# Parts of Q and K written to DRAM once, two groups later, and read twice by the fills of the stacks

## The chip, the cores and the metric

The kernel runs on one core of a Trainium2 chip. The metric is the device time of one launch in microseconds, as the median of several runs. All data are float32 in DRAM. The engines that matter are TensorE (PE in the profile: matrix products, with weight loads as PEld), VectorE (DVE), ScalarE (ACT), GpSimd (POOL) and SyncE (SP), whose instructions here issue DMA transfers. ScalarE can issue DMA transfers too. The 16 DMA engines of the core carry them out.

## The reference

The reference is one post-norm transformer layer on x of shape (8, 1024, 256): attention with 16 heads of 16 elements and a fixed bias, then a feed-forward layer with ternary weights and a low-rank addition.

```python
Q = split_heads(x @ Wq.T + bq); K = split_heads(x @ Wk.T + bk); V = split_heads(x @ Wv.T + bv)
scores = einsum('bhqd,bhkd->bhqk', Q, K) / sqrt(16) + prior_lambda * _gaussian_mask(1024)
out = einsum('bhqk,bhkd->bhqd', softmax(scores), V)
x = layernorm(x + out.reshape(8, 1024, 256) @ Wo.T + bo)
h = bitlinear(x, w_fc) + gate * (x @ v.T @ fast_b.T @ u.T)
x = layernorm(x + bitlinear(relu(h) ** 2, w_proj))
```

## The kernel before

Products are made at float32 precision out of a faster, shorter type (float32r). Each of Q and K is split into two parts, a rounded part and the rest, held in the tile `two` (L629 to L631: ScalarE rounds, GpSimd subtracts). A score is then one product over 64 rows: for each of 16 elements of the head, four rows pair the parts of K with the parts of Q in all four ways. In K the four rows are part 0, part 1, part 0, part 1. In Q they are part 0, part 1, part 1, part 0.

These 64 rows are the *stacks* (L290): for each pair of heads `pr` and each member `a` of the pair, one tile for K and one for Q, 64 partitions of 1024 float32 values. Member `a` = 0 uses partitions 0 to 63, member 1 partitions 64 to 127. The other partitions hold zeros, and two rows for the row maxima. There are two slots, so that one head group of four heads is used while the next one's stacks are filled.

The way from `two` to a stack goes through DRAM. `write_parts` (L199) writes the parts into `parts_of`, a DRAM tile of 128 rows (8 heads of 16 elements), four copies and 1024 columns; `fill_one` (L313) reads the 16 rows of one head, four copies each, into the 64 partitions of a stack. `fill_stack` (L321) makes the eight fills of a head group, K and Q in turn, all on the SP queue. Only the very first head group is filled in halves, part of it on ScalarE's queue, and its parts are written for the low 64 rows first (L244 to L339).

The main loop (L1508) runs over 512 groups, 16 for a head group and 64 for a batch. A group g makes the exponentials of two tiles (`exp_scores`, L751) and the maximum of rows for the scores that are used 12 groups later (`max_scores`, L652, with `max_row` on VectorE, L674). Every 16 groups, at the loop's head, `fill_stack` asks for the next head group; its first scores are made 4 groups later. Every 8 groups `set_max` (L688) turns the maxima, and sends them through DRAM (`rows`) into the Q stacks by one write and four copies (L702, L709). The exponentials need them 3 groups later. All engines follow the order in which the program is written (L1632 to L1637); among the DMAs of one queue this order holds as well.

Beside that, a list of pieces of other work is spread over the groups: making Q and K of the next heads (`queries_keys`, L602), V, and the feed-forward layer of the batch before. `defer(n, f)` (L383) puts f at the end of the group n groups later. At the end of a head group the weighted sums go to DRAM (`raw_o` and `sums`, L812, L815). When the third and the fourth head group of a batch are done, `normalize` (L822) fetches the sums (`den`, one group later), inverts them on VectorE (three groups later, L834), writes them back (`back`, L836) and reads them repeated 16 times (`rec`, L841: the source lists 8 rows, each repeated for 16 partitions).

Of the kernel before, what the change touches and what calls it, by code (L numbers as in the profile page):

```python
# [10 lines left out]
F32 = mybir.dt.float32  # L11
# [6 lines left out]
P = 128  # L18
HD = 16
HG = 4  # L20
VW = HD + 1
HALF = 512
# [21 lines left out]
def tile_postln_layer(  # L44
# [20 lines left out]
    nc = tc.nc  # L65
    B, L, D = x.shape
# [29 lines left out]
    def big(name):  # L96
        return epool.tile([P, 2 * HALF], F32, tag="e", name=name)
# [12 lines left out]
    for name, w in (("k", wk), ("q", wq), ("v", wv), ("o", wo)):  # L110
        t = big(f"raw_{name}")[:, : NDC * D].rearrange("p (c d) -> p c d", d=D)
# [3 lines left out]
    for name, src in (("k", bk), ("q", bq)):  # L115
        t = cpool.tile([P, NDC], F32, tag=f"b{name}", name=f"b{name}")
# [74 lines left out]
    parts_of, made = {}, {}  # L191

    def new_parts(name, b, c):
        parts_of[name, b, c] = dpool.tile(
            [P, 4, L], F32, tag=f"parts_{name}", name=f"parts_{name}_{b}_{c}"
        )
        return parts_of[name, b, c]

    def write_parts(name, t, two, half, rows=slice(0, P)):  # L199
        to, two = t[rows, :, ts(half, HALF)], two[rows].bitcast(F32)  # L200
        nc.sync.dma_start(to[:, :2], two)
        if name == "k":
            nc.sync.dma_start(to[:, 2:], two)
        else:
            nc.sync.dma_start(to[:, 2, :], two[:, 1, :])
            nc.sync.dma_start(to[:, 3, :], two[:, 0, :])

    def first_part(name, half, two):
        pt = bank0(f"p{name}_0_0_{half}")
# [20 lines left out]
    for name in "kq":  # L230
        new_parts(name, 0, 0)
# [4 lines left out]
    two = {}  # L236
# [5 lines left out]
    low, high = slice(0, P // 2), slice(P // 2, P)  # L242
    two["k", 0] = first_part("k", 0, two_tile("k", 0, p1, "two"))
    write_parts("k", parts_of["k", 0, 0], two["k", 0], 0, low)  # L244
    first_turn(1)
    two["q", 0] = first_part("q", 0, two_tile("q", 0, epool, "e"))
    write_parts("q", parts_of["q", 0, 0], two["q", 0], 0, low)
    two["k", 1] = first_part("k", 1, two_tile("k", 1, p1, "o0"))
    write_parts("k", parts_of["k", 0, 0], two["k", 1], 1, low)
    two["q", 1] = first_part("q", 1, two_tile("q", 1, p1, "o1"))  # L250
    turn_weights("v", nc.vector.tensor_copy)
# [17 lines left out]
    def split_prior():  # L269
# [7 lines left out]
        for k in range(1, PIECES):  # L277
# [12 lines left out]
    stack = {  # L290
        (name, s, pr, a): cpool.tile(
            [P, L], F32R, tag=f"{name}{s}{pr}{a}", name=f"st_{name}_{s}_{pr}_{a}"
        )
        for s in range(SLOTS)
        for pr in range(NP)
        for a in range(2)
        for name in "qk"
    }

    for (name, s, pr, a), t in stack.items():  # L300
        if a:
            nc.gpsimd.memset(t[: P // 2].bitcast(F32), 0.0)
        if name == "k":
            at = 0 if a else P // 2
# [3 lines left out]
    for n in range(2):  # L308
        t = cpool.tile([P, NB, NH, VW], F32, tag=f"v{n}", name=f"v_{n}")
# [3 lines left out]
    def fill_one(name, G, pr, a, queue, cols=slice(0, L)):  # L313
        (b, g), s = divmod(G, NG), G % SLOTS
        at, src = P // 2 * a, HD * ((g % 2) * HG + 2 * pr + a)
        queue.dma_start(
            stack[name, s, pr, a][at : at + P // 2, cols].bitcast(F32),
            parts_of[name, b, g // 2][src : src + HD, :, cols].rearrange("p l n -> (p l) n"),
        )

    def fill_stack(G):  # L321

        assert made.get((G // NG, G % NG // 2)) == 2 * NHALF
        for pr in range(NP):
            for a in range(2):
                for name in "kq":
                    fill_one(name, G, pr, a, nc.sync)

    halves_of_q = slice(0, HALF), slice(HALF, L)
    for pr in range(NP):  # L330
        for a in range(2):
            fill_one("k", 0, pr, a, nc.sync)
            fill_one("q", 0, pr, a, nc.scalar, halves_of_q[0])
# [49 lines left out]
    def defer(n, f):  # L383
        later.append((now + n, f))
# [192 lines left out]
    def has_xT(b, half):  # L577
        return turned.get((b, half)) == 2 * NDC

    def values(b, bank):  # L580
# [18 lines left out]
            (0.86, lambda t=t: piece(t), 1, lambda t=t: has_xT(b, t // QB)) for t in range(NB)  # L599
        ]  # L600

    def queries_keys(b, c, bank):  # L602


        st = {}

        def piece(name, half, k):
            t = new_parts(name, b, c) if half == 0 and k == 0 else parts_of[name, b, c]
            pt = bank(f"p{name}_{b}_{c}_{half}_{k}")
            for dc in range(NDC):  # L610
                nc.tensor.matmul(  # L611
                    pt,
                    wT[name][:, dc, ts(c, P)],
                    xT[:, dc, ts(2 * half + k, D)],
                    start=(dc == 0),
                    stop=(dc == NDC - 1),
                )

            def empty():
                bias = bcol[name][:, c : c + 1]  # L620
                if k == 0:
                    st["full"] = p2.tile(
                        [P, HALF], F32, tag="rl", name=f"full{name}_{b}_{c}_{half}"
                    )
                full = st["full"]
                nc.scalar.activation(full[:, ts(k, D)], pt, AF.Identity, bias=bias)  # L626
                if k == 0:
                    return
                two = p1.tile([P, 2, HALF], F32R, tag="two", name=f"two{name}_{b}_{c}_{half}")  # L629
                nc.scalar.copy(two[:, 0, :], full)  # L630
                nc.gpsimd.tensor_sub(two[:, 1, :], full, two[:, 0, :].bitcast(F32))  # L631
                made[b, c] = made.get((b, c), 0) + 1
                write_parts(name, t, two, half)

            return empty

        return [
            (
                0.86,
                lambda name=name, half=half, k=k: piece(name, half, k),  # L640
                1,
                lambda half=half: has_xT(b, half),
            )
            for half in range(NHALF)
            for name in "kq"
            for k in range(2)
        ]
# [762 lines left out]
    def jobs_of(b):  # L1410


        qk = queries_keys(b, 1, misc)
        load, early_xv, ahead = [], [], []
        if b + 1 < B:
            load = [(0.0, lambda: load_x(b + 1, 0), 0)]
            xs, vs = transpose_x(b + 1, misc), values(b + 1, misc)
            early_xv, ahead = xs[:4] + vs[: NB // 2], xs[4:]
            ahead = ahead + queries_keys(b + 1, 0, misc) + vs[NB // 2 :]
# [88 lines left out]
    for g in range(-LEAD, total + 1):  # L1508
# [43 lines left out]
        if g < 0:  # L1552

            n = g + LEAD + 1 - (done >= QSTEP - 1)
# [55 lines left out]
    def bank(name):  # L1610
        return whole_bank(name)[:, :D]
# [73 lines left out]
```

## Time and profile before

| what | value |
|---|---|
| median of 3 runs | 2144.75 us (2143.95 to 2145.74) |
| the profiled execution, its own time | 2146.07 us |
| its span, first to last instruction | 2144.3 us |
| busy share: TensorE, VectorE, ScalarE, GpSimd | 97%, 73%, 67%, 43% |
| DMA: bytes moved | 193.55 MB, mean 90 GB/s |
| HBM written | 85.69 MB |
| fills of the stacks on SP | 128 for K, 124 for Q, of 256 KB |
| writes of the parts of K on SP | 60 of 512 KB, 8 of 256 KB |
| writes of the parts of Q on SP | 64 of 256 KB, 30 of 512 KB, 8 of 128 KB |

The busy shares are means over the whole span. Times on the timeline start with the span. A line of the timeline gives the start, the time taken, the engine, the line of the kernel, the operation and its tiles; for a DMA on SPq the time taken is that of the issue, not of the transfer. In a bracket stands how long the engine was idle before, and what ended it. In the line of a window stand its bounds and length, then the busy time of TensorE, weight loads, VectorE, ScalarE and GpSimd, each with its instructions, the granted clock of TensorE, the DMA share and GB/s. In the DMA view each digit is the busy share of the 16 DMA engines in one of 40 slices of the window, in tenths.

### The profile page before, as it was taken

How to read it: one execution, taken by the hardware profiler on the slowest of the kernel's cores; microseconds unless marked ns; L12 is line 12 of the kernel's file. 1: busy time of each engine (PE TensorE's matmuls, PEld its weight loads, DVE VectorE, ACT ScalarE, POOL GpSimd, SP SyncE). 2: the span in 40 equal slices, each digit the busy share in tenths (PEclk: the TensorE clock that was granted, in tenths of full speed). 3: DMA queues.
4: the chain of work that ended last, by engine and by line, in shares of the span. 5: the costliest groups of instructions: out<-in, count | busy, mean ns of one | idle time of the engine just before them, and what ended most of it. 6: DMA issues, size and time to landing. Idle time of an engine off the chain costs nothing.

```text
span 2144.3 us, 38970 instructions
## 1 busy us (share of the span) xinstructions
PE 2073.6 (97%) x14200; PEld 1200.6 (56%) x14200; DVE 1568.2 (73%) x2909; ACT 1440.2 (67%) x2155; POOL 917.2 (43%) x1075
## 2 busy tenths in 40 slices
PE   6999999999999999999999999999999999999997
PEld 3444445555555555556555555555555555555657
DVE  6777777777777777777777777777777777777736
ACT  2566666766777667667777767677676766766754
POOL 5044332344324453345533445335543445455444
PEclk9999999999999999999999999999999999999999
DMA  6423334223433124423233223422343321422010
GB/s 192 124 76 112 77 88 143 68 62 78 124 103 107 56 60 121 137 73 84 72 133 110 76 70 99 132 86 58 78 124 120 90 70 49 138 74 56 23 47 20
DMA packets 110725, 193.55 MB, mean 90 GB/s; under 512 B 21149, under 2 KB 50253, under 8 KB 110533
## 3 DMA queue, kind: packets, MB, share of 16 engines
q1 hardware_dynamic: 109116, 189.48, 31.3%
q8 instruction: 112, 1.84, 0.4%
q10 hardware_dynamic: 1416, 1.58, 0.2%
q14 instruction: 81, 0.66, 0.1%
HBM read 105.19 MB, written 85.69 MB: 89 GB/s over the span
## 4 chain that ended last, share of the span: by engine, by line
PE 80%; DVE 11%; POOL 3%; DMA 3%; issue 2%; ACT 1%; SPq 0%; DVEq 0%; POOLq 0%; ACTq 0%
PE e L761 22%; PE av L791 19%; PE s L665 16%; DVE junk L677 8%; PE misc L1065 5%; PE misc L611 4%; PE misc L1100 4%; PE misc L584 2%; PE misc L991 2%; PE e L742 1%; PE misc L1072 1%; DVE st L949 1%; DMA parts_k<-twok 1%; PE misc L1025 1%; PE misc L558 0%
## 5 line engine op out<-in xcount | busy, mean ns | idle before, releaser
L677 DVE CUSTOM_DVE_ANT_0 junk<-s,wide 128x1024 f32<-128x1024 f32 x1024 | 1249.1, 1220 | 484.1 <-PE s L665 440.5
L776 ACT ACTIVATE exp<-e 128x1024 f32<-128x1024 f32 x1024 | 1027.6, 1024 | 549.2 <-PE e L761 371.3
L761 PE MATMUL e<-st_q,st_k 66*128 66x512 f32 (+1 forms) x2048 | 618.0, 423 | 0.7 <-DMA st_q<-rows 0.4
L791 PE MATMUL av<-exp,v 128*17 128x512 f32 x4096 | 539.8, 598 | 0.0
L761 PEld LDWEIGHTS e<-st_q,st_k 66*128 66x128 f32 (+1 forms) x2048 | 344.0, 189 | 292.8 <-ACT exp L776 95.3
L665 PE MATMUL s<-st_k,st_q 64*128 64x512 f32 x2048 | 393.9, 446 | 40.1 <-DVE pm L677 25.9
L665 PEld LDWEIGHTS s<-st_k,st_q 64*128 64x128 f32 x2048 | 165.3, 185 | 172.3 <-DVE pm L677 88.6
L775 DVE TENSOR_TENSOR e<-e,wide 128x372 f32<-128x372 f32 (+2 forms) x376 | 190.1, 506 | 38.2 <-PE e L761 35.7
L1083 POOL TENSOR_TENSOR rl<-rl 128x512 f32<-128x512 f32 x112 | 116.7, 1042 | 234.1 <-ACT hi L1082 221.1
L791 PEld LDWEIGHTS av<-exp,v 128*17 128x17 f32 x4096 | 68.1, 95 | 185.7 <-issue 184.3
L742 PEld LDWEIGHTS <-ident_q 96*32 96x32 bf16 x2112 | 64.3, 97 | 162.9 <-issue 159.0
L1085 POOL TENSOR_TENSOR lo<-rl,hi 128x512 fp32r<-128x512 f32 x112 | 143.8, 1284 | 8.8
L1120 POOL TENSOR_TENSOR r<-r,sp_row 128x256 f32<-128x256 f32 x56 | 41.1, 734 | 212.0 <-ACT r L1119 212.0
L594 POOL TENSOR_TENSOR v<-v,bv_row 128x256 f32<-128x256 f32 x64 | 44.0, 689 | 191.9 <-ACT v L593 191.9
L1065 PE MATMUL misc<-xhi,wfT 128*128 128x256 f32 x448 | 117.0, 284 | 0.4 <-ACT fullq L626 0.2
L1065 PE MATMUL misc<-xlo,wfT 128*128 128x256 f32 x448 | 115.0, 280 | 0.0
L1100 PE MATMUL misc<-wpT,lo 128*128 128x256 f32 x448 | 112.0, 282 | 2.6 <-POOL lo L1085 2.6
L1100 PE MATMUL misc<-wpT,hi 128*128 128x256 f32 x448 | 114.3, 288 | 0.0
L631 POOL TENSOR_TENSOR twok<-fullk,twok 128x512 fp32r<-128x512 f32 x30 | 38.6, 1287 | 145.3 <-ACT twok L630 143.6
L1078 ACT ACTIVATE rl<-misc,s_fc 128x256 f32<-128x256 f32 x224 | 94.0, 475 | 0.9 <-POOL lo L1085 0.9
L1065 PEld LDWEIGHTS misc<-xhi,wfT 128*128 128x128 f32 x448 | 84.4, 188 | 10.6 <-ACT fullk L626 2.4
L1100 PEld LDWEIGHTS misc<-wpT,lo 128*128 128x128 f32 x448 | 85.3, 190 | 6.7 <-POOL lo L1085 3.2
(233 smaller groups left out, 2351.9 us busy)
## 6 DMA issues: line engine op xcount, KB each, us to landing
st_k<-parts_k SPq DMA_DIRECT2D x128, 256.0 KB
st_q<-parts_q SPq DMA_DIRECT2D x124, 256.0 KB
parts_k<-twok SPq DMA_DIRECT2D x60, 512.0 KB
parts_q<-twoq SPq DMA_DIRECT2D x64, 256.0 KB
parts_q<-twoq SPq DMA_DIRECT2D x30, 512.0 KB
x<-in_L_attn_x_dram SPq DMA_DIRECT2D x16, 512.0 KB
raw_o<-avs SPq DMA_DIRECT2D x248, 32.0 KB
rec<-back SPq DMA_DIRECT2D x30, 256.0 KB
```

The lines of the kernel that those rows point to most:

```text
L611: nc.tensor.matmul(pt, wT[name][:, dc, ts(c, P)], xT[:, dc, ts(2 * half + k, D)], start=(dc == 0), stop=(dc == NDC - 1),)
L665: nc.tensor.matmul(pair[a][:, kh, :], stack["q", s, pr, a][rows, ts(blk, P)], stack["k", s, pr, a][rows, ts(kh, HALF)], start=True, stop=True,
L677: nc.vector.tensor_tensor_reduce(out=junk, in0=t.rearrange("p k n -> p (k n)"), in1=wide[:, LEFT - P * blk : LEFT - P * blk + L], scale=1. ...
L761: nc.tensor.matmul(t[:, a, :], stack["k", s, pr, a][rows, ts(blk, P)], stack["q", s, pr, a][rows, ts(h, HALF)], start=not by_pe, stop=True ...
L775: nc.vector.tensor_add(part, part, add.to_broadcast([P, 2, hi - lo]))
L776: nc.scalar.activation(e, t.rearrange("p a n -> p (a n)"), AF.Exp)
L791: nc.tensor.matmul(av[32 * j : 32 * j + HD + 1, :], v_bufs[b % 2][:, blk, g * HG + j, : HD + 1], es[j // 2][:, ts(j % 2, HALF)], start=(n ...
L1065: nc.tensor.matmul(ph, wfT[:, dc, ts(hc, P)], st[k2][:, dc, :], start=(dc == 0 and k2 == "xhi"), stop=False,)
L1078: nc.scalar.activation(rl[:, ts(k, n)], ph, AF.Relu, scale=s_fc[:, hc : hc + 1])
L1083: nc.gpsimd.tensor_mul(rl, rl, rl)
L1085: sub(lo, rl, hi.bitcast(F32))
L1100: nc.tensor.matmul(py, st[k][:, hc, ts(i, P)], wpT[:, hc, :], start=(hc == 0 and k == "hi"), stop=(hc == NHC - 1 and k == "lo"),)
```

## The change

The parts are written once. `parts_of` holds two copies in place of four, and `write_parts` becomes one DMA, for K in place of two and for Q in place of three. The fills read the parts twice, and the order of the 64 rows changes: K's are now part 0 and part 1 of all 16 elements, and the same 32 rows once more; Q's are part 0 of each element twice, then part 1 of each element twice. Each row of K still meets the row of Q that it has to. A K fill is one DMA whose source has the repeat outermost, a count of 2 with a step of 0, then 32 rows. A Q fill becomes two DMAs of 32 rows, whose source has 16 rows outermost, each repeated twice.

The write in the loop moves: in place of standing right behind the subtraction, it is put off to the end of the group two groups later, or to the point just before ScalarE writes into `two` again, if that comes first.

```diff
-            [P, 4, L], F32, tag=f"parts_{name}", name=f"parts_{name}_{b}_{c}"
+            [P, 2, L], F32, tag=f"parts_{name}", name=f"parts_{name}_{b}_{c}"
...
     def write_parts(name, t, two, half, rows=slice(0, P)):
-        to, two = t[rows, :, ts(half, HALF)], two[rows].bitcast(F32)
-        nc.sync.dma_start(to[:, :2], two)
-        if name == "k":
-            nc.sync.dma_start(to[:, 2:], two)
-        else:
-            nc.sync.dma_start(to[:, 2, :], two[:, 1, :])
-            nc.sync.dma_start(to[:, 3, :], two[:, 0, :])
+        nc.sync.dma_start(t[rows, :, ts(half, HALF)], two[rows].bitcast(F32))
...
-        queue.dma_start(
-            stack[name, s, pr, a][at : at + P // 2, cols].bitcast(F32),
-            parts_of[name, b, g // 2][src : src + HD, :, cols].rearrange("p l n -> (p l) n"),
-        )
+        part = parts_of[name, b, g // 2][src : src + HD, :, cols]
+        n, to = part.shape[-1], stack[name, s, pr, a]
+        if name == "k":
+            both = part.rearrange("p l n -> (p l) n").unsqueeze(0).to_broadcast([2, 2 * HD, n])
+            queue.dma_start(to[at : at + P // 2, cols].bitcast(F32), both)
+            return
+        for l in range(2):
+            rows = slice(at + 2 * HD * l, at + 2 * HD * (l + 1))
+            queue.dma_start(
+                to[rows, cols].bitcast(F32), part[:, l : l + 1, :].to_broadcast([HD, 2, n])
+            )
...
+    unwritten = []
+
+    def write_pending():
+        while unwritten:
+            unwritten.pop(0)()
...
                 if k == 0:
                     return
+                write_pending()
                 two = p1.tile([P, 2, HALF], F32R, tag="two", name=f"two{name}_{b}_{c}_{half}")
                 nc.scalar.copy(two[:, 0, :], full)
                 nc.gpsimd.tensor_sub(two[:, 1, :], full, two[:, 0, :].bitcast(F32))
                 made[b, c] = made.get((b, c), 0) + 1
-                write_parts(name, t, two, half)
+                unwritten.append(lambda: write_parts(name, t, two, half))
+                defer(2, write_pending)
```

In the built program a DMA of 256 KB that fills a K stack has on its source side the counts 2, 32, 1024 and on its side of the stack 64 and 1024. Every DMA carries one of eight completion semaphores in turn, and waits for the DMA that carried the same one before it. A fill of a head group is 12 DMAs on SP in place of 8.

## Prediction

> **What bounds the kernel now.** I read the page's engine lines first, then the table by windows (busy time, granted clock and DMA share of a stretch), then the SyncE queue (SP) on the timeline, then the DMA view of two short windows.
>
> ```profile
> PE 2073.6 (97%) x14200; PEld 1200.6 (56%) x14200; DVE 1568.2 (73%) x2909; ACT 1440.2 (67%) x2155; POOL 917.2 (43%) x1075
> ```
>
> ```profile
> 340.00:617.00 277.00, 273.27 (x1887) 156.38 (x1886) 205.66 (x378) 191.12 (x284) 112.50 (x126) 1.00 0.31 89
> 26.00:28.00 2.00, 0.95 (x3) 0.50 (x4) 0.00 (x0) 0.00 (x0) 0.00 (x0) 0.50 0.87 209
> 28.00:30.00 2.00, 2.00 (x6) 1.17 (x7) 1.23 (x2) 0.00 (x0) 0.00 (x0) 0.50 1.02 312
> ```
>
> TensorE is busy 273.3 of 277 us once the loop runs, so DMA is hidden there. Little can be won; every wait that a late DMA puts on TensorE, or on an engine that feeds it, is paid. The last two lines belong to the start: after 8 us without matmuls the granted clock was 0.50 until 30.4.
>
> How much is hidden shows on SP. Three fills of the stacks, each with what stands behind it:
>
> ```profile
> 22.89 2.41 SPq L316 DMA_DIRECT2D st_k<-parts_k  x4
> 26.74 0.76 PE L665 MATMUL s<-st_k,st_q 64*128 64x512 f32 x1 [8.10 <-DMA st_k<-parts_k]
> ...
> 617.04 0.49 SPq L316 DMA_DIRECT2D st_k<-parts_k  x1
> 643.42 0.33 SPq L702 DMA_DIRECT2D rows<-both  x1
> 646.18 1.13 SPq L709 DMA_DIRECT2D st_q<-rows  x4
> 647.43 0.62 ACT L630 CAST twoq<-fullq 128x512 fp32r<-128x512 f32 x1
> 651.50 1.19 PE L761 MATMUL e<-st_q,st_k 66*128 66x512 f32 x4
> ...
> 744.21 0.50 SPq L316 DMA_DIRECT2D st_k<-parts_k  x1
> 760.44 0.40 SPq L1114 DMA_DIRECT2D out_dram<-r  x1
> 760.89 0.47 SPq L829 DMA_DIRECT2D den<-sums  x1
> 765.19 0.33 SPq L836 DMA_DIRECT2D back<-den  x1
> ...
> 808.04 0.49 SPq L316 DMA_DIRECT2D st_k<-parts_k  x1
> 817.74 0.54 SPq L815 DMA_DIRECT2D sums<-avs  x1
> 821.44 0.34 SPq L829 DMA_DIRECT2D den<-sums  x1
> 827.74 0.34 SPq L836 DMA_DIRECT2D back<-den  x1
> ```
>
> A fill comes every 16 groups (63.8 us from 744.21 to 808.04). The score matmuls use it about 21 us later. Behind a fill, SP carries the row maxima (26.4 us after it, needed by the matmul at +34.5) or the sums whose reciprocal VectorE takes just before `back` (+21.0 and +19.7).
>
> How fast a fill moves, and how a read of repeated rows spreads: the DMA view of 617 to 631 us (40 slices of 0.35 us) holds a fill of 2 MB; that of 269.5 to 275.5 (0.15 us each) holds one `rec<-back`, 256 KB, whose source lists 8 rows and repeats each 16 times.
>
> ```profile
> DMA  9999849300093999998999999999999998971000
> GB/s 363 421 386 392 135 158 363 82 0 0 0 176 117 398 269 293 246 199 176 211 246 234 234 246 222 222 199 211 222 281 222 211 211 176 193 194 35 0 0 0
> ```
>
> ```profile
> DMA  0000000000063554564442400000000000000000
> GB/s 27 27 0 27 0 27 0 0 0 0 0 150 150 205 218 191 205 177 150 150 96 55 109 0 0 0 0 0 0 0 0 0 0 0 0 0 0 0 0 0
> ```
>
> With all 16 DMA engines busy the fill, which writes 64 partitions, moves about 215 GB/s, 13.4 an engine; the transfers just ahead of it moved 363 to 421, some 25 an engine. `rec` alone never holds more than 4 to 6 tenths of the engines, at up to 205 to 218 GB/s: 8 of 16, at 25.6 each.
>
> **The change, part by part.**
>
> *Fewer writes.* K's two writes become one, Q's three become one: 102 writes fewer on SP, some 33 MB less, and most of the 251 us that SP waited at L201 for GpSimd go. In the loop all that lies beside TensorE's work: nothing, with its 98.7% as cover. At the start the first fill waits for a write issued at 17.55 (VectorE's end) instead of 18.54: -1.0 us.
>
> *The Q fill.* It becomes two DMAs of 32 rows, on ScalarE's queue too. Outermost there are still 16 rows, and the four more issues of about 0.55 us on SP precede nothing needed within 6 us: nothing. At the start ScalarE waits for TensorE anyway.
>
> *The K fill.* Its source now has the count 2 outermost (the repeat), then 32 rows. By `rec`, whose outermost 8 held 8 engines, it runs on 2: 131 KB on each. The price of one lies between 5.1 us (25.6 GB/s, `rec`) and 9.8 us (13.4 GB/s, the present fill); below 5.1 there is no row. I take 9.8, because the present fill is nearest: the same source, the same 64 partitions, the same 4 KB rows. Whether two engines alone reach more, no row shows. Four K fills queue up on the two engines. The first packet starts 1.3 us after the issue (two engines' packets follow `rec`'s issue at 269.77 by about as much), so the fourth lands T = 1.3 + 39.0 = 40.3, say 41, after the first is issued. The bound by `rec`, with the Q rows in between, is T = 24.
>
> The rule that weighs here stands in the Trainium skill, DMA: Bandwidth & Descriptors, "Why a DMA increments its semaphore by 16 and not by 1": the engine count is the largest up to 16 that divides the outermost counts of both sides. `rec`'s 8 agrees, and it gives 2 for K. At that page's 27 GiB/s an engine, T would be about 21 and the kernel, by an estimate, 2290 us. The skill's SBUF — State Buffer, "Door 1: The DMA port swizzle", has partitions p and p + 32 behind one port, which speaks for the slow rate and so for 2800; the 215 GB/s agrees.
>
> *Who waits.* In the built program a DMA carries one of eight semaphores in turn and waits for the DMA eight before it. The fourth K fill is the tenth DMA of a fill; so the 18th stands still until T, and SP with it. Which one that is, the instruction order of the changed program tells:
>
> - Fills at a batch's first head group (batches 1 to 7): the 18th is `sums`. `den` follows 3.7 us later (817.74 to 821.44) and `back` 4.3 after that (760.89 to 765.19): 41 + 8.0 = 49.0 in place of 19.7. VectorE stands in the reciprocal for 29.3 us, and the row maxima, score buffers and TensorE behind it. 7 x 29.3 = 205.
> - Fills at the last head group (batches 0 to 6): the 18th is the output (once a weight load), then `den`: 41 + 0.45 + 4.3 = 45.8 in place of 21.0. 7 x 24.8 = 174.
> - The 17 others: mostly `rows`, at 41 in place of 26.4; its copies go out 2.8 later and land 1.3 after (the chain has one at 1.32): 45.1, needed at 34.5. 17 x 10.6 = 180.
>
> *The later write.* `two` has one buffer. ScalarE's next copy into it waits for a write that now stands two groups later on SP. Where the next piece comes just two groups on (13 places by the order of the program), write and copy meet. The write lands about 4.0 us after its issue, by the chain:
>
> ```profile
> 331.56 3.99 DMA parts_k<-twok
> 335.64 0.62 ACT twoq L630
> ```
>
> Six of them follow a second-head-group fill: the write stands behind the copies of the row maxima and lands at 41 + 8.3 = 49.3, while ScalarE wants to copy at 30.4 (647.43): 18.9 in place of 10.6, 6 x 8.3 = 50. Seven stand in the group of the maxima: 8.8 less 1.3 of ScalarE's idle third of a 4 us group, 7 x 7.5 = 52.
>
> *The start.* The first scores need two K fills: 21.9 + 1.3 + 19.5 + 0.3 = 43.0 in place of 26.7, +16.3. The fifth group of scores, 11 us on at VectorE's 2.76 a group, needs the fourth: 62.9 against 54.0, +8.9. Together 25.
>
> *Clock and slack.* At the start 3.7 us after the gap ran at 0.50, a loss of 1.8; 31 long gaps: 56. Against that each of 44 waits is eaten into by some 2 us (VectorE's idle 27% of a group, and three score buffers): -88.
>
> Sum: 205 + 174 + 180 + 102 + 25 + 56 - 88 = 654. The profiled execution took 2146.07 us (span 2144.3), 1.3 above the median of the three; 2144.75 + 654 = 2799, say 2800.
>
> **The rivals.**
>
> *Two engines at full rate* (T = 24). For it: `rec`'s 25.6 GB/s in its first slices. Against it: the last slices of `rec` fall to 55 to 150 GB/s. Then 7 x (12.3 + 7.8) = 141; the `rows` at 26.4 pass untouched; later writes 6 x 4.3 + 52 = 78; start 8; clock 14 x 1.8 = 25; slack 27 x -2 = -54: 198, so 2343.
>
> *The K fill spreads over 16 engines.* For it: destination and bytes are as before. Against it: `rec`. T stays near 11, `back` isn't late, and the 13 copies on ScalarE are left: 78 - 26 = 52, so 2196.
>
> *Faster.* As the last, with a single write, half the bytes, landing before ScalarE's copy. It decides if T is under 11.7 (19.7 less 8.0) and the write lands in under 2 us, against the 3.99 of a pair. Gain: 1.0 at the start and the 1.5 that TensorE lacked between 300 and 340 us (38.48 of 40.00): 2142.
>
> *More than the sum:* the long waits hold up other loads behind the two engines as well. Each us more of T costs 14 + 17 + 6 = 37 us; T = 46 gives 2985.
>
> **How the numbers follow.** Chances: 58% for the slow rate (its own range, T 38 to 44: 2690 to 2910), 27% two engines at full rate, 5% sixteen engines, 3% faster, 7% more than the sum. 2310 to 2990 leaves out the cases near 2150 to 2200 and the far end, and holds about 8 in 10. A measurement tells 0.2% from no change: 3% faster, 2% within it, 95% slower.
>
> **What would show it.** The DMA share at a tenth or two for most of 40 us after a fill (if right), nines for 10 us (if not); on SP the 18th DMA of a fill 41 us after the first; VectorE idle before the reciprocal by 25 to 29 us; ScalarE waiting for `parts_k<-twok`; granted clock below 1.00 after each gap. Wrong would be: fills landing within 12 us, or TensorE's lost time lying elsewhere than behind the fills.

## The result, and the profile after

The changed kernel takes 2493.03 us (median of 4 runs, 2489.40 to 2494.79), the kernel before 2145.24 us (4 runs, 2143.95 to 2147.75). The ratio is 1.1616, with a 95% interval of 1.1598 to 1.1633: the change costs 348 us. The profiled execution of after has a span of 2489.9 us, 345.6 more than that of before. Line numbers are shifted against before: K fills stand at L315, Q fills at L319, the write of the parts at L200, `sums` at L825, `den` at L839, the reciprocal at L844, `back` at L846, `rows` at L712.

The page of after, span and engine lines, with the granted clock below:

```profile
span 2489.9 us, 38996 instructions
PE 2138.7 (86%) x14200; PEld 1227.1 (49%) x14200; DVE 1570.0 (63%) x2909; ACT 1438.1 (58%) x2155; POOL 916.4 (37%) x1075
PEclk8798998899989989899989999899998999899999
```

The work is the same (14200 matmuls, 2909 instructions on VectorE), and VectorE, ScalarE and GpSimd are busy for as long as before. TensorE's share falls from 97% to 86%, and the 65 us more that it is busy (2138.7 against 2073.6) come with a granted clock of 0.93 in place of 0.99.

SP on the timeline of after, one fill at a batch's first head group:

```profile
966.61 0.55 SPq L315 DMA_DIRECT2D st_k<-parts_k  x1
967.20 1.22 SPq L319 DMA_DIRECT2D st_q<-parts_q  x2
968.53 0.53 SPq L315 DMA_DIRECT2D st_k<-parts_k  x1
969.10 1.17 SPq L319 DMA_DIRECT2D st_q<-parts_q  x2
970.37 0.53 SPq L315 DMA_DIRECT2D st_k<-parts_k  x1
970.94 6.71 SPq L319 DMA_DIRECT2D st_q<-parts_q  x2
977.75 0.53 SPq L315 DMA_DIRECT2D st_k<-parts_k  x1
978.32 5.28 SPq L319 DMA_DIRECT2D st_q<-parts_q  x2
983.64 0.59 SPq L104 DMA_DIRECT2D x<-in_L_attn_x_dram  x1
984.34 6.77 SPq L822 DMA_DIRECT2D raw_o<-avs  x4
995.49 0.56 SPq L825 DMA_DIRECT2D sums<-avs  x1
998.26 0.34 SPq L839 DMA_DIRECT2D den<-sums  x1
1000.64 0.34 SPq L846 DMA_DIRECT2D back<-den  x1
1008.96 0.33 SPq L712 DMA_DIRECT2D rows<-both  x1
```

The fill's twelve DMAs are no longer issued in one go: the pairs of Q at 970.94 and 978.32 take 6.71 and 5.28 us, because one of each pair waits for an earlier K fill to land. `sums`, the 18th DMA, stands until 28.9 us after the first, and `back` follows at +34.0; before it was at +19.7.

The DMA view of after, 1118 to 1148 us, 40 slices of 0.75 us, with the next fill in it:

```profile
DMA  0018627211126111531124111831111231112000
GB/s 0 0 11 197 180 71 235 77 38 38 38 66 186 44 49 55 126 126 49 55 98 148 38 55 55 229 93 55 49 55 49 74 112 55 55 55 68 33 25 22
```

A digit of 1 with 38 to 55 GB/s is two engines at work. The higher digits between are the rows of Q on 16 engines. The two engines are busy from slice 2 to the end, some 28 us; before, nines stood for 10 us.

The waits of after: engine, line, what it waited for, then total us, times, longest.

```profile
POOL twoq L640 <- ACT twoq L639: 182.5, 28, 28.9
PE s L675 <- DVE pm L687: 179.7, 68, 18.7
DVE den L844 <- DMA den<-sums: 170.1, 13, 15.6
ACT twoq L639 <- DMA parts_k<-twok: 110.9, 18, 17.8
PE s L675 <- ACT exp L786: 57.3, 15, 15.6
```

VectorE waits before the reciprocal for `den`, 13.1 us on the mean (170.1 / 13), which before was no wait that shows, and TensorE waits for VectorE behind it (179.7 us against 25.9 before). ScalarE waits 110.9 us for the write of `two` (2.2 before).

SP's own waits in after; the last line is `sums`, held by a K fill:

```profile
SPq L319 <- DMA st_k<-parts_k: 189.5, 63, 4.9
SPq L822 <- DMA st_k<-parts_k: 119.0, 31, 5.0
SPq L712 <- DMA st_k<-parts_k: 50.2, 12, 4.9
SPq L825 <- DMA st_k<-parts_k: 35.0, 8, 4.4
```

Where the lost time lies shows when each stretch from one fill to the next is set against the same stretch of before (63.5 us in the steady part):

| stretch | extra us in all | each |
|---|---|---|
| up to the fill at the second head group's start (118.62 us before, 146.85 after) | 28.2 | |
| behind the fill of a batch's first head group | 157.3 | 22.5 (7) |
| behind the second | 44.2 | 5.5 (8) |
| behind the third | 18.5 | 2.3 (8) |
| behind the last | 97.4 | 13.9 (7) |
| sum | 345.6 | |

The fills of all these stretches are alike, and yet the loss isn't spread evenly. In batches 2 to 6 the stretch behind the third head group's fill is 0.1 to 0.5 us longer than before, while those behind the first and the last, where `sums` or `den` and then `back` stand on SP behind the fill, are 11 to 25 us longer.

### The profile page after: what moved, and what is told of

It reads as the page before. It is cut to its first block, busy times and chain, and to the rows that moved or that the text cites. A ratio compares the mean times of both kernels' runs of the same rounds, so it can differ in the third digit from the quotient of the medians.

```text
span 2489.9 us, 38996 instructions
## 1 busy us (share of the span) xinstructions
PE 2138.7 (86%) x14200; PEld 1227.1 (49%) x14200; DVE 1570.0 (63%) x2909; ACT 1438.1 (58%) x2155; POOL 916.4 (37%) x1075
## 5 line engine op out<-in xcount | busy, mean ns | idle before, releaser
L786 ACT ACTIVATE exp<-e 128x1024 f32<-128x1024 f32 x1024 | 1026.1, 1024 | 754.8 <-PE e L771 417.1
L771 PE MATMUL e<-st_q,st_k 66*128 66x512 f32 (+1 forms) x2048 | 631.6, 431 | 16.5 <-DVE pm L687 14.8
L675 PE MATMUL s<-st_k,st_q 64*128 64x512 f32 x2048 | 415.7, 459 | 262.2 <-DVE pm L687 179.7
L801 PE MATMUL av<-exp,v 128*17 128x512 f32 x4096 | 560.1, 619 | 0.0
L771 PEld LDWEIGHTS e<-st_q,st_k 66*128 66x128 f32 (+1 forms) x2048 | 353.2, 194 | 323.1 <-ACT exp L786 82.5
L675 PEld LDWEIGHTS s<-st_k,st_q 64*128 64x128 f32 x2048 | 175.4, 190 | 400.9 <-DVE pm L687 235.1
L844 DVE RECIPROCAL den<-den 128x64 f32<-128x64 f32 x15 | 8.3, 552 | 170.1 <-DMA den<-sums 170.1
L710 POOL TENSOR_TENSOR both<-neg,both 16x128 fp32r<-16x128 f32 x64 | 28.8, 450 | 214.0 <-ACT neg L709 214.0
L640 POOL TENSOR_TENSOR twoq<-fullq,twoq 128x512 fp32r<-128x512 f32 x30 | 38.4, 1280 | 182.5 <-ACT twoq L639 182.5
```

What stands on the lines that cost most here:

```text
L675: nc.tensor.matmul(pair[a][:, kh, :], stack["q", s, pr, a][rows, ts(blk, P)], stack["k", s, pr, a][rows, ts(kh, HALF)], start=True, stop=True,
L771: nc.tensor.matmul(t[:, a, :], stack["k", s, pr, a][rows, ts(blk, P)], stack["q", s, pr, a][rows, ts(h, HALF)], start=not by_pe, stop=True ...
L786: nc.scalar.activation(e, t.rearrange("p a n -> p (a n)"), AF.Exp)
L801: nc.tensor.matmul(av[32 * j : 32 * j + HD + 1, :], v_bufs[b % 2][:, blk, g * HG + j, : HD + 1], es[j // 2][:, ts(j % 2, HALF)], start=(n ...
```

## The experiments

Three theories remained. A: the K fills run on two DMA engines, and the SP queue with all that stands behind them is held until they land. B: the later write, which ScalarE's next copy into `two` has to wait for, is the larger part. C: reading the parts twice, in the new order of rows, is slow in itself.

**The repeat inside.** The same kernel, with the count of 2 behind the 32 rows of K instead of ahead of them; the rows of Q are put where they meet the same rows of K. Bytes and repeats stay.

```diff
-            both = part.rearrange("p l n -> (p l) n").unsqueeze(0).to_broadcast([2, 2 * HD, n])
+            both = part.rearrange("p l n -> (p l) n").unsqueeze(1).to_broadcast([2 * HD, 2, n])
...
-            rows = slice(at + 2 * HD * l, at + 2 * HD * (l + 1))
+            rows = slice(at + l, at + P // 2, 2)
```

> The changed kernel with the K fill's repeat moved inside: its source counts 32 rows outermost, then 2, and the Q rows are placed so that each still meets its K row. DMAs, bytes and their order are those of the changed kernel; only the outermost count goes from 2 to 32. Theory A (a count of 2 outermost puts the K fill on two DMA engines; it lands at about 28 us and SP stands behind it): the fills land within 12 us as before, the reciprocal's wait for den (170 us in all) goes, and what the later write costs is left: 2160 to 2195 us. Theory B (the later write is the larger cost): at least 2380. Theory C (reading the same rows twice, or the new order of rows, is slow in itself): about 2490.

It took 2197.82 us (2195.94 to 2204.36), 1.0235 times the kernel before (1.0219 to 1.0251), just above the upper end that theory A gave. No wait before the reciprocal is left. What is left is the later write. ScalarE's wait:

```profile
ACT twoq L639 <- DMA parts_k<-twok: 58.5, 19, 6.8
```

Of the 49.8 us by which the span is longer, 44.4 lie behind the seven fills of a first head group.

**The write at once.** The changed kernel with its fills, but the one write issued right behind the subtraction.

```diff
-                unwritten.append(lambda: write_parts(name, t, two, half))
-                defer(2, write_pending)
+                write_parts(name, t, two, half)
```

> The changed kernel with the write of the parts put back right behind the subtraction; the fills stay as changed (repeat outermost). Theory A: only ScalarE's waits for the write get shorter (110.9 us in all in the changed kernel, not all of it paid): 2400 to 2475 us, and den still waits about 170 us. Theory B: 2145 to 2250. Theory C: about 2490.

2447.0 us (2440.79 to 2451.27), ratio 1.138 (1.1358 to 1.1402). The two waits:

```profile
DVE den L843 <- DMA den<-sums: 177.4, 13, 16.0
ACT twoq L639 <- DMA parts_k<-twok: 58.9, 10, 15.8
```

VectorE's wait for `den` stays in full. The fills alone carry some 300 of the 348 us; theory B falls. ScalarE still waits ten times, though the write is issued at once: my reading is that it now stands behind a held queue, and in the kernel with both undone, further down, no wait of `two` for `parts_k` is left.

**The kernel before with the later write alone.** Two writes for K and three for Q, as before, but put off like the change does.

```diff
+    unwritten = []
+
+    def write_pending():
+        while unwritten:
+            unwritten.pop(0)()
+
...
+                write_pending()
                 two = p1.tile([P, 2, HALF], F32R, tag="two", name=f"two{name}_{b}_{c}_{half}")
...
-                write_parts(name, t, two, half)
+                unwritten.append(lambda: write_parts(name, t, two, half))
+                defer(2, write_pending)
```

> The kernel before with nothing but the later write: two groups later, or just before ScalarE writes into the buffer again; four copies in DRAM and fills as before. Theory A: ScalarE waits at 13 places by 4 to 9 us, partly hidden: 2165 to 2200 us. Theory B: at least 2400. Theory C: within 0.2% of before.

2234.91 us (2230.93 to 2236.24), ratio 1.0399 (1.0385 to 1.0413): 35 us above the upper end expected. The wait of ScalarE:

```profile
ACT twoq L637 <- DMA parts_k<-twok: 79.9, 20, 7.2
```

It stands 20 times, where the first experiment has 19, but takes 4.0 us on the mean in place of 3.1; here two or three writes must land before the copy, there one. So the later write costs 87 us with the writes of before (2234.91 less 2148.07 for before in the same runs), and some 50 with the single write. This was mis-sized in the expectation; it doesn't raise the part that the late write has in the change, where the write is single.

**Both undone: the repeat inside and the write at once.** What is left of the change is the single write and the double read, in an order of rows that again is new.

> Both together: repeat inside and the write at once, so that of the change only the single writes and the double reading are left. Theory A: 2135 to 2150 us, no clear difference from before beyond about 1 us at the start. Theory B: the same. Theory C: about 2490, or at least well above before.

2144.61 us (11 runs, 2142.70 to 2146.83) beside 2148.07 for before: 0.9985 (0.9976 to 0.9994). The page's engine line, and the DMA view of one fill (932.5 to 947.5 us, 40 slices of 0.375 us):

```profile
PE 2075.1 (97%) x14200; PEld 1201.9 (56%) x14200; DVE 1568.0 (73%) x2909; ACT 1439.6 (67%) x2155; POOL 915.9 (43%) x1075
```

```profile
DMA  0005979799799999999999999999996000000000
GB/s 0 0 0 98 218 284 361 142 175 230 229 339 219 186 164 175 251 262 240 219 186 175 197 218 295 219 186 175 164 202 181 0 0 11 5 5 0 0 0 0
```

With the repeat inside, the fill is a row of nines over some 10 us, as in before. Theory C falls. The 33.6 MB that are no longer moved (159.99 against 193.55 MB) bring 0.15%, at the limit of what can be told from nothing. The parts add up: 302 us for the fills (2447.0 less 2144.61), 53 for the later write (2197.82 less 2144.61), together 355 against 348.

**Two and three of the four K fills on two engines.** Does the loss come from the moment at which the queue is let go, or does each byte through two engines cost its share? On top of the last kernel, only some of the K fills of a head group get the repeat outermost: those of the first pair of heads, then also the third one.

```diff
+        outermost = pr == 0
         if name == "k":
-            both = part.rearrange("p l n -> (p l) n").unsqueeze(1).to_broadcast([2 * HD, 2, n])
+            once = part.rearrange("p l n -> (p l) n")
+            both = (
+                once.unsqueeze(0).to_broadcast([2, 2 * HD, n])
+                if outermost
+                else once.unsqueeze(1).to_broadcast([2 * HD, 2, n])
+            )
```

The kernel with three has `outermost = pr == 0 or a == 0`; in both, the rows of Q follow those of K.

> Writes at once; of the four K fills of a head group the first two have the repeat outermost (two DMA engines), the last two have it inside (16 engines). Known: none of four 2144.6 us, four of four 2447.0 us. Theory of the held queue: a K fill with the repeat outermost takes about 6.8 us with its Q rows beside it, the second lands about 15 us after the first issue, and the queue is let go before the inverse of the sums is due (19.7 us in the kernel before), with at most some 4 us on each of 14 fills: 2145 to 2215. Rival, each byte through two engines costs its share wherever it stands: half of the 302 us, 2280 to 2310.

> As the last, with three of the four K fills on two engines. Theory of the held queue: the third lands about 22 us after the first issue, the sums go out behind it, the write of the inverse stands at about 27 us in place of 19.7: 14 x 8 = 112 us, and the row maxima (due at 26.4) hardly later: 2230 to 2300. Rival, the cost goes with the bytes: three quarters of 302 us, 2360 to 2385.

Two: 2332.97 us, ratio 1.0878 (1.0847 to 1.0909). Three: 2380.12 us, ratio 1.1105 (1.1077 to 1.1133). Both are far above what the theory of the held queue gave. The second is inside the rival's range, the first above it, so neither set of numbers holds. SP on the timeline of the kernel with two, from a fill at 896.79 on:

```profile
896.79 0.54 SPq L321 DMA_DIRECT2D st_k<-parts_k  x1
...
901.14 8.52 SPq L329 DMA_DIRECT2D st_q<-parts_q  x2
909.76 0.54 SPq L321 DMA_DIRECT2D st_k<-parts_k  x1
910.35 6.93 SPq L329 DMA_DIRECT2D st_q<-parts_q  x2
917.32 0.59 SPq L104 DMA_DIRECT2D x<-in_L_attn_x_dram  x1
...
920.79 0.56 SPq L834 DMA_DIRECT2D sums<-avs  x1
923.51 0.34 SPq L848 DMA_DIRECT2D den<-sums  x1
925.83 0.34 SPq L855 DMA_DIRECT2D back<-den  x1
```

I had put the landing of the second K fill at 15 us. The last DMA of the fill is the 12th. It waits for the second K fill, the 4th DMA, and goes out at 916.77 (the second of the two Q issues from 910.35 on), 20.0 us after the first: two K fills with 16-engine transfers beside them took 20 us. So the input was wrong. Whether the mechanism holds is told by setting the lateness of `back` against the loss of the same stretch, both against before and on the mean over the 14 fills of first and last head groups (the differences are taken before rounding):

| K fills on two engines | `back` later, us | stretch longer, us | difference |
|---|---|---|---|
| none (write at once) | -0.2 | 0.0 | 0.2 |
| two of four | 7.7 | 9.9 | 2.1 |
| three of four | 10.2 | 12.3 | 2.0 |
| four of four (write at once) | 13.9 | 16.1 | 2.2 |

The loss is the lateness of `back` and 2 us more, in all three. The 2 us show in TensorE's own time: in these 14 stretches it is busy 2.3, 2.2 and 2.3 us longer than before (63.80, 63.70 and 63.81 us on the mean against 61.54), with the granted clock below 1.00 in each. One such stretch, before and with four of four (write at once):

```profile
808.04:870.28 62.24, 61.90 (x430) 35.57 (x429) 45.67 (x82) 45.57 (x67) 26.24 (x27) 1.00 0.44 135
956.43:1034.68 78.25, 63.49 (x429) 35.95 (x428) 45.63 (x82) 45.54 (x67) 26.15 (x27) 0.91 0.28 85
```

The reciprocal's wait follows the lateness too; the two lines are of the kernel with two, and of that with three:

```profile
DVE den L853 <- DMA den<-sums: 96.4, 13, 9.6
```

```profile
DVE den L853 <- DMA den<-sums: 128.9, 13, 12.3
```

That is the held queue: 138 of 182 us and 172 of 231 us of the longer spans lie behind these 14 fills. In neither kernel does the stretch behind the third head group's fill in batches 2 to 6 grow by more than 0.6 us, though it has the same two-engine fills; a cost that goes with the bytes wherever they stand would show there. What fell is the price of a fill.

**The price of a K fill by itself.** To the kernel before, 16 reads are added behind its last output. The first 12 each wait for the one ahead.

```diff
+    flat = parts_of["k", B - 1, 1].rearrange("p l n -> (p l) n")
+    to = stack["k", 0, 0, 0].bitcast(F32)
+
+    def twice(n):
+        return flat[:n].unsqueeze(0).to_broadcast([2, n, L])
+
+    apart = flat[:80].rearrange("(a b) n -> a b n", a=2)[:, :32]
+    for _ in range(2):
+        nc.sync.dma_start(to[:64], twice(32))
+        nc.sync.dma_start(to[:64], flat[:64])
+        nc.sync.dma_start(to[:32], twice(16))
+        nc.sync.dma_start(to[slice(0, 64, 2)], twice(16))
+        nc.sync.dma_start(to, twice(64))
+        nc.sync.dma_start(to[:64], apart)
+    for s in range(2):
+        for pr in range(NP):
+            nc.sync.dma_start(stack["k", s, pr, 1][64:].bitcast(F32), twice(32))
```

> The kernel before, with 16 reads behind its last output, the first 12 each waiting for the one before to land, nothing else moving: twice over (1) the K fill of the change, two engines into rows 0-31 and 32-63; (2) the K fill of before, 16 engines into the same 64 rows; (3) two engines into rows 0-15 and 16-31; (4) two engines into rows 0, 2, ... 30 and 32, 34, ... 62; (5) two engines into rows 0-63 and 64-127; (6) as (1) but the two engines read different rows of DRAM; then four of (1) back to back into four stacks. The run is some 100 us longer for it. If rows 32 apart disturb each other: (1), (4), (6) run at about 33 GB/s (300 ns a packet of 4 KB, as in the first us of the fills of the changed kernel), (3) and (5) at 50 (159 ns). If it is the reading of one DRAM row by two engines: (6) alone at 50. If the slow stretch came from the other transfers beside it: all of the two-engine ones at 50 to 52 GB/s, 256 KB in 5.1 us, and four in about 21 us. (2) at 215 GB/s, 1.2 us, in all cases.

There is one run of it, 2259.96 us beside 2152.91 for before. SP on the timeline, where each start but the first follows the landing of the read ahead (L1640 to L1645 are the six kinds in the order above):

```profile
2148.19 0.57 SPq L1640 DMA_DIRECT2D st_k<-parts_k  x1
2157.53 0.50 SPq L1641 DMA_DIRECT2D st_k<-parts_k  x1
2161.17 0.67 SPq L1642 DMA_DIRECT2D st_k<-parts_k  x1
2166.34 0.52 SPq L1643 DMA_DIRECT2D st_k<-parts_k  x1
2171.80 0.49 SPq L1644 DMA_DIRECT2D st_k<-parts_k  x1
2184.42 0.49 SPq L1645 DMA_DIRECT2D st_k<-parts_k  x1
2192.58 0.48 SPq L1640 DMA_DIRECT2D st_k<-parts_k  x1
```

From issue to landing the K fill of the change takes 9.34 us (2157.53 less 2148.19), that of before 3.64. Half of it on two engines takes 5.17 (rows 0 to 31) or 5.46 (rows 32 apart), twice the bytes 12.62, and the K fill from different rows of DRAM 8.16. The second round gave 9.22, 3.49, 5.06, 5.29 and 12.76 for the first five kinds. From 5.17 us for 131 KB and 12.62 for 524 KB, two engines move 52.8 GB/s once they run (393 KB in 7.45 us); at that rate the K fill would have taken 7.65. It takes 1.7 us more. In the two rounds 14 and 17 of its 64 packets of 4 KB take 290 ns and more, most others about 159. Of the three guesses none holds: rows 32 apart do it no harm at L1643, one DRAM row read by two engines does none at L1644, and yet the transfer isn't at full rate alone. Why a single K fill has slow packets stays open. With the reads queued up, the second L1645 and the four of L1648, they are nearly gone (10 of 320). The DMA view of 2228.9 to 2258.2 us, 40 slices of 0.73 us:

```profile
DMA  0101011111111111111111111111111111111000
GB/s 0 22 22 39 34 45 39 45 50 45 56 56 50 50 56 50 50 56 56 45 56 56 50 50 56 50 50 56 56 45 56 56 50 50 56 50 50 28 0 0
```

At 50 GB/s a K fill in a queue of K fills costs 5.2 us.

## Why the prediction was right or wrong

Slower was right, and 2493 lies within the range; the forecast of 2800 was 307 us too high. That it lies within owes something to luck: it is in neither of the two cases that the range was drawn around (2690 to 2910 for the slow rate, 2343 for two engines at full rate), and terms that were too high stood beside a slack that took off too much. T is, as in the prediction, the time from the first issue of a fill to the landing of its fourth K fill. Step by step:

**Two engines.** Right, and the base of all the rest. With the count of 2 outermost the DMA view shows ones at about 50 GB/s; with the same count inside it shows nines. The Trainium skill, DMA: Bandwidth & Descriptors, "Why a DMA increments its semaphore by 16 and not by 1", takes the largest number up to 16 that divides the outermost counts of both sides; that gives 2, as seen.

**The price of one K fill is the term that was mis-sized most:** "I take 9.8, because the present fill is nearest". It made T = 41. The 18th DMA went out at +28.9. By the issues that waited for them, the four K fills of that fill had landed at +10.5, +16.5, +23.3 and +28.9: the price was nearly right for the first, and the three behind it took about 6 us each. Same rows, same 64 partitions, same packets of 4 KB; what I left out is that the 13.4 GB/s an engine came with all 16 engines writing at once. When SP is held, little else moves, and two engines in a queue reach about 25 each, as in `rec`, the other bound. I took a rate that 16 engines shared for a property of the place that is written. The truth lay between the bounds: 7.65 or so alone at full rate and 9.34 measured from issue to landing, 5.2 in a queue, and about 7 in the kernel (28.9 us less 1.3, by four) with the rows of Q in between. The kernel with two of four shows the other side: where 16-engine transfers remain beside them, two K fills took 20 us. The skill's SBUF — State Buffer, "Door 1: The DMA port swizzle", which I had set down for the slow rate, isn't seen in two engines' writes to rows 32 apart (5.46 against 5.17 us).

**Who waits.** Right in place. At a first head group `sums` is the 18th DMA and stands until T. `den` and `back` then came faster than I had it (2.8 and 2.4 us, not 3.7 and 4.3), so that `back` is 14.3 us late on the mean, 11.8 at a last head group, and VectorE stood before the reciprocal for 13.1 us, not 25 to 29. With T = 28.9 my own terms give 7 x 17.2 = 120 and 7 x 12.7 = 89; the stretches lost 157 and 97, the later write included. The 17 other fills, priced at 180, cost nearly nothing where the loop runs steadily: at T = 28.9 the copies of the row maxima land at 33.0, before the 34.5 at which they are needed. The 62.7 us measured behind second and third head groups lie mostly in the first two batches and the last.

**The later write.** Its term was 102 us, about twice too high: with the fills of the change it costs 46 (2493.03 less 2447.0), without them 53. For the seven places in the group of the maxima I had 7.5 us each; in the first experiment the seven first-head-group stretches lost 6.3 each. The six others, at 8.3, shrank with T: the middle batches lost 2 to 4.

**The start.** 25 forecast, 28.2 found, but by another way. The first fill went out at 20.02 in place of 22.89, 2.9 us earlier where I had 1.0. TensorE's first score came at 30.82 in place of 26.74, 4.1 later; the next ones, which need the second K fill, at 35.73 in place of 27.81, 7.9 later where I had 16.3. The rest is the stretch behind it, with a wait of 17.8 us of ScalarE for the write of `two` behind the held queue among it.

**Clock and slack.** I let each wait be eaten into by 2 us of slack. Nothing was eaten: with the write at once the 14 stretches lost the whole lateness of `back`, and 2.2 us on top, which is about the clock's price, forecast at 1.8 a gap. (At the start of before I misread the clock: the window from 30 to 34 us has a mean of 0.80, so 0.50 lasted until 31.6 and not 30.4, and the loss there was 2.4.) With T = 28.9 and all else as I had it, the sum would have been 120 + 89 + 0 + (6 x 6.8 + 7 x 7.5 = 93) + 13 at the start + 14 x 1.8 for the clock - 27 x 2 of slack = 286, so 2431. Without the slack 2485, against 2493 measured, but the parts don't fit one by one: 287 priced in the 14 stretches (with seven of the later writes and the clock) where 255 were lost, 41 behind the second and third head groups where it was 63, 13 at the start where it was 28. This is also why the rival "two engines at full rate", 2343 at T = 24, was too low: T was 5 us longer (from two to three to four of four, the span grew by about 20 us for each us by which `back` was later; my 37 for each us of T was too much), and it took the same slack off each wait.

**The rivals.** "Sixteen engines" and "faster" are refuted for this kernel. The kernel with the repeat inside and the later write is what "sixteen engines" described: 2197.82, where it gave 2196. That close a number is partly chance: it was priced as 13 waits of ScalarE, six of 4.3 us and seven of 7.5, less 26 of slack, and there were 19 of 3.1 us on the mean. "Faster" needed T under 11.7 and a short write; with the repeat inside and the write at once the gain is 0.15%.

## What to carry to other kernels

In these kernels the count that stands outermost in a source decided how many DMA engines carried it: 2 with the repeat outermost, 16 with the 32 rows outermost. So a repeat of 2 belongs behind the rows, not ahead of them; the same bytes then cost 302 us less here. A slow transfer that nobody needs soon can still be dear, because the DMAs behind it on the queue wait for its semaphore: count to the DMA that stands still, and ask what is needed from there on. When a rate is taken from a profile, look at how many engines shared it.

## What the runs showed that I had not expected

- A K fill on two engines is slower alone than in a queue (9.34 us from issue to landing, against 5.2 each in a row), and its slow packets, 300 ns against 159, are found neither with rows 32 apart alone nor with one DRAM row read twice alone.
- The first two K fills took longer when only they were on two engines: with two of four the issue of the fill's last DMA, which waits for the second K fill, ended at +20.5 us (910.35 and 6.93, less 896.79), with four of four at +17.0 (978.32 and 5.28, less 966.61). In the first case two K fills on 16 engines ran beside them.
- A late `back` costs its lateness and 2 us more, at 8, 10 and 14 us alike; TensorE's busy time grew by as much, at a lower granted clock.
